# Full-array matmuls written as four tiles of 32 columns, and the last 64-row block of a down projection moved behind the scores

## The chip, the cores and the metric

The kernel runs on one core of one Trainium2 chip. The metric is the device time of one execution in microseconds (us); the kernel before takes 3293.29 us, the median of 6 runs between 3290.56 and 3295.43. The engines are named as in the profile: PE (TensorE, the matrix unit), DVE (VectorE), ACT (ScalarE), POOL (GpSimd) and SP (SyncE, which issues most DMAs). PEld is the loading of weights into PE's array, SPq is SP's queue.

## The reference

Two blocks follow each other on x of shape (8, 1024, 256), all in fp32. The first is attention with compressed keys and values. The second, which the change touches, is a two-layer transformer with attention in windows of 128 tokens:

```python
def _layer(x, wqkv, qs, ksc, wo, lg, lb, w1, b1, w2, b2):
    b, n, _ = x.shape
    h = shift_token(x)                      # second half of the features comes from the token before
    q, k, v = jnp.split(h @ wqkv, 3, axis=-1)
    q, k, v = (to_heads(q), to_heads(k), to_heads(v))   # 8 heads of 64
    q = l2norm(q) * qs
    k = l2norm(k) * ksc
    q, k = rotary_xpos(q, k)
    o = local_attention(q, k, v)            # each window sees itself and the one before
    x = x + o.transpose(0, 2, 1, 3).reshape(b, n, INNER) @ wo
    h = layernorm(shift_token(x)) * lg + lb
    a, g = jnp.split(h @ w1 + b1, 2, axis=-1)
    return x + (a * gelu(g)) @ w2 + b2      # hidden width 682 = 5 x 128 + 42
```

## The kernel before

The first phase (to about 967 us) computes the first block and leaves its result in DRAM (`x2d`). It already writes its dense products through a helper `times` (L199 to L201), which makes four matmuls of 32 output partitions each out of one product. The second phase, the function `local`, holds the two layers.

`local` makes 16 passes, one for each layer and batch row, layer 0 for all eight rows first. A pass has NT = 8 windows of 128 tokens and two chunks of CH = 512 tokens. One loop over steps (`for step in range(windows + LAG)`) advances everything by one window, and the order in which PE, DVE, ACT and POOL get their instructions is the order in which this loop emits them (`manual_schedule`). SP's order is left to a scheduler. In step `step`, in this order:

- `both` (window step - 4, L983): DVE adds the exponentials of two windows for the softmax sums.
- `qk` (window step, L886): the query and key products, 2 x 2 matmuls of 128 x 512 into one of two double banks (`pair`). ACT squares them, DVE and POOL apply the rotary tables and the norms.
- `transposes` (window step - 1, L926): DVE transposes blocks, and SP writes them to DRAM (`z`) and reads them back into the ring `qkT`.
- `v` (L913): the value product, into a bank of the pool `mm`, copied out by ACT.
- a unit of the MLP, `next(units)`
- `ahead`: on the last windows of a pass, the next pass's stream of x is loaded and, in layer 0, normalised by DVE (L788).
- `values` (window step - 4): the products with the exponentials, `o` (L999), and their sums `s` (L1007, in a bank of `mm`), both in tiles of 32 columns. DVE then takes the reciprocal of s (L1011), reduces s over its free axis for a check (L1015), scales o (L1016) and reduces the reciprocal (L1020).
- `scores` (window step - 3, L958): tiles of 64 rows and 32 columns into the two `pair` banks; ACT takes the exponentials (L964), POOL masks them.
- `output` in every second step: the output projection `psw` (L1032) into a bank of `mm`, added to x by DVE (L1036), stored by SP.
- a second unit of the MLP

The MLP of a chunk has eight units, so it takes four steps. The first five hold the up projection (`up`, L1115, tiles `ag`), with gelu on ACT and the gate on DVE (L1128, tile `hid`). The sixth makes the last 42 hidden columns: their gate and value share one product, and the result is laid in `rest_hid` as two blocks of 64 rows (L1142), one for each half of the chunk. The seventh is the down projection: `sums`, two banks of `mm`, gather 40 products over the five full blocks (L1156) and then the products with the two 64-row blocks (L1162). DVE adds both banks to x (L1168), and SP stores x, in layer 0 to `xs` (L1170). In layer 1, DVE adds the input `xt` first (L1174), and SP stores to `out`. The eighth scales the next chunk.

The pool `psum3`, tag `mm`, has three banks. A new tile gets a bank that is free in the order of the program, and its first matmul waits until the last reader of the old tile has finished. The seventh unit falls on the place between `v` and `values`, so the order in such a step is: pair, pv, psy with its rest, o, s, scores, psw.

Of the kernel before, what the change touches and what calls it, by code (L numbers as in the profile page):

```python
# [32 lines left out]
ALU = mybir.AluOpType  # L33
# [3 lines left out]
P = 128  # L37
# [20 lines left out]
DEPTH, HEADS, DH, WINDOW = 2, 8, 64, 128  # L58
INNER = HEADS * DH
# [3 lines left out]
CH = 512  # L63
# [19 lines left out]
def preln_mla_local_kernel(  # L83
# [27 lines left out]
    nc = tc.nc  # L111
# [541 lines left out]
    ST = CH // P  # L653
    NF = HID // P
# [3 lines left out]
    def local(ctx: ExitStack, verdict):  # L658
# [4 lines left out]
        p1 = ctx.enter_context(tc.tile_pool(name="l1", bufs=1))  # L663
        p2 = ctx.enter_context(tc.tile_pool(name="l2", bufs=2))

        ppair = [ctx.enter_context(tc.tile_pool(name="pair0", bufs=1, space=PSUM))]
        psum = ctx.enter_context(tc.tile_pool(name="psum3", bufs=3, space=PSUM))
        ppair.append(ctx.enter_context(tc.tile_pool(name="pair1", bufs=1, space=PSUM)))
# [7 lines left out]
        rest_hid = p1.tile([P, CH // 2], F32, name="rest_hid")  # L676
# [90 lines left out]
        def load_x2(b, n):  # L767
            xt = p1.tile([P, ST, D], F32, tag="x2", name=f"x2_{b}_{n}")
            nc.sync.dma_start(xt, x2d[b][:, ST * n : ST * n + ST])
            return xt  # L770
# [94 lines left out]
        class Pass:  # L865
# [14 lines left out]
            def qk(self, i):  # L880
                key, w = self.key(i), self.w
                A, S = w["cos"], w["sin"]
                qk = next(turns).rearrange("p (n j) (m d) -> p n (j m) d", n=2, d=DH)
                for n in range(2):
                    for c in range(2):
                        nc.tensor.matmul(  # L886
                            qk[:, n].rearrange("p h d -> p (h d)"), self.left(i)[c],
                            w["qkv"][:, c, n * INNER : (n + 1) * INNER], start=(c == 0), stop=(c == 1),
                        )
                sq = p1.tile([P, 2, HEADS, DH], F32, tag="sq", name=f"sq{key}")  # L890
                nc.scalar.activation(sq, qk, AF.Square)  # L891
                t1 = p1.tile([P, 2, HEADS, DH], F32, tag="t1", name=f"t1{key}", bufs=2)
                nc.vector.tensor_tensor(t1, qk, A[:, i].unsqueeze(2).to_broadcast([P, 2, HEADS, DH]), ALU.mult)  # L893
                t2 = p1.tile([P, 2, HEADS, DH], F32, tag="t2", name=f"t2{key}")
                for lo, hi in ((0, H), (H, 0)):
                    nc.vector.tensor_tensor(  # L896
                        t2[:, :, :, lo : lo + H], qk[:, :, :, hi : hi + H],
                        S[:, i, :, lo : lo + H].unsqueeze(2).to_broadcast([P, 2, HEADS, H]), ALU.mult,
                    )
                nc.gpsimd.tensor_tensor(t1, t1, t2, ALU.add)  # L900
                ss = small.tile([P, 2, HEADS], F32, tag="ss", name=f"ss{key}")
                nc.vector.tensor_reduce(ss, sq, AX.X, ALU.add)
                nc.vector.tensor_scalar(ss, ss, 1e-24, None, ALU.max)
                rn = small.tile([P, 2, HEADS], F32, tag="rn", name=f"rn{key}")
                rsqrt(rn.rearrange("p i h -> p (i h)"), ss.rearrange("p i h -> p (i h)"), 2 * HEADS)
                nc.gpsimd.tensor_tensor(t1, t1, rn.unsqueeze(3).to_broadcast([P, 2, HEADS, DH]), ALU.mult)  # L906
                self.rot[i] = t1

            def v(self, i):
                key = self.key(i)  # L910
                pv = psum.tile([P, INNER], F32, tag="mm", name=f"pv{key}")
                for c in range(2):
                    nc.tensor.matmul(  # L913
                        pv, self.left(i)[c], self.w["qkv"][:, c, 2 * INNER :], start=(c == 0), stop=(c == 1)
                    )
                self.vs[i] = p1.tile([P, INNER], F32, tag="v", name=f"v{key}", bufs=6)
                evac(self.vs[i], pv)

# [105 lines left out]
            def output(self, n):  # L1024

                oT = self.oTs.pop(n)
                x_, y, key = self.x_, self.y, f"{self.b}_{self.l}"
                two = slice(2 * n, 2 * n + 2)
                ps = psum.tile([P, 2, D], F32, tag="mm", name=f"psw{key}_{n}")
                for i in range(2):  # L1030
                    for c in range(4):
                        nc.tensor.matmul(  # L1032
                            ps[:, i, :], oT[:, c, i * P : (i + 1) * P], self.w["o"][:, c, :],
                            start=(c == 0), stop=(c == 3),
                        )
                nc.vector.tensor_tensor(x_[:, two], ps, x_[:, two], ALU.add)  # L1036

                rows = slice(2 * n * P, (2 * n + 2) * P)
                nc.sync.dma_start(y[rows, :P].rearrange("(t p) d -> p t d", p=P), x_[:, two, :P])
                rows = slice(2 * n * P + 1, (2 * n + 2) * P + 1)  # L1040
                nc.sync.dma_start(y[rows, P:].rearrange("(t p) d -> p t d", p=P), x_[:, two, P:])
                m, o = divmod(2 * n + 2, ST)
                if o == 0:
                    self.hs[m - 1] = p2.tile([P, ST, D], F32, tag="h", name=f"h{key}_{m - 1}")
                    rows = slice((m - 1) * CH, m * CH)
                    nc.sync.dma_start(self.hs[m - 1], y[rows].rearrange("(t p) d -> p t d", p=P))
# [2 lines left out]
        made = {}  # L1049
        chunks = [(n, m) for n in range(len(passes)) for m in range(NCH)]  # L1050
        ds, found = {}, {}

        def look_at_chunk(k):
            if k < len(chunks):
# [41 lines left out]
        def mlp():  # L1096


            w = load_mlp(0)
# [7 lines left out]
            for k, (q, n) in enumerate(chunks):  # L1107
# [4 lines left out]
                def up(i):  # L1112
                    ps = psum.tile([P, CH], F32, tag="mm", name=f"ag{key}_{i}")
                    for c in range(2):
                        nc.tensor.matmul(  # L1115
                            ps.rearrange("p (s a t) -> p s a t", a=4, t=32), w["1"][:, c, i, :],
                            d[:, c],
                            start=(c == 0), stop=(c == 1),
                        )
                    return ps  # L1120

# [24 lines left out]
                norm_chunk(k + 1)  # L1146
                turn_chunk(k + 1)
                yield
                if l + 1 == DEPTH:
                    xt = load_x2(b, n)  # L1150
                sums = [psum.tile([P, 2, D], F32, tag="mm", name=f"psy{key}_{g}") for g in range(2)]
                for g, ps in enumerate(sums):
                    for t in range(2):
                        cols = slice((2 * g + t) * P, (2 * g + t + 1) * P)
                        for i in range(NF):
                            nc.tensor.matmul(  # L1156
                                ps[:, t, :], hid[:, i, cols], w["2"][:, i, :], start=(t == i == 0), stop=False
                            )
                for t in range(2):
                    for g, ps in enumerate(sums):  # L1160
                        rows = slice(64 * g, 64 * g + 64)
                        nc.tensor.matmul(  # L1162
                            ps[:, t, :], rest_hid[rows, t * P : (t + 1) * P], w["2"][rows, NF, :], start=False,
                            stop=(t == 1),
                        )
                for g, ps in enumerate(sums):
                    part = slice(ST * n + 2 * g, ST * n + 2 * g + 2)
                    nc.vector.tensor_tensor(x_[:, part], ps, x_[:, part], ALU.add)  # L1168
                    if l + 1 < DEPTH:
                        nc.sync.dma_start(xs[b][:, part], x_[:, part])  # L1170
                    else:
                        rows = slice(n * CH + 2 * g * P, n * CH + (2 * g + 2) * P)
                        both = xt[:, 2 * g : 2 * g + 2]
                        nc.vector.tensor_tensor(both, x_[:, part], both, ALU.add)  # L1174
                        nc.sync.dma_start(out[b, rows].rearrange("(t p) d -> p t d", p=P), both)
                yield
                if k + 1 < len(chunks) and made[chunks[k + 1][0]].l > l:
                    w = load_mlp(l + 1)
# [26 lines left out]
        def each(step, name, back):  # L1205
            j = step - back
            if 0 <= j < windows:
                n, i = divmod(j, NT)
                getattr(made[n], name)(i)

        E = mybir.EngineType
        with tc.manual_schedule(engines={E.PE, E.DVE, E.Activation, E.Pool}):
            for step in range(windows + LAG):
# [18 lines left out]
                    ahead(n + 1)  # L1232
                each(step, "values", 4)
                each(step, "scores", 3)
                j = step - 6
                if 0 <= j < windows and j % 2 == 0:
                    made[j // NT].output(j % NT // 2)
# [8 lines left out]
                if i >= NT - 5 and step < windows:  # L1246
                    got = ahead(n + 1)
                    if got:
                        ready[n + 1] = got
            for _ in units:  # L1250
                pass

        ok = p1.tile([P, 2, B * DEPTH * NT], F32, name="okl")
        for m, top in enumerate((HIGH, 1 / LOW)):
# [612 lines left out]
```

## Time and profile before

| | |
|---|---|
| median of 6 runs | 3293.29 us |
| the profiled execution | 3296.12 us |
| its span, first to last instruction | 3294.3 us |
| granted clock of PE, mean | 0.993 |
| PE busy | 3199.9 us (97%), 33762 matmuls |
| DVE busy | 2668.8 us (81%) |
| ACT, POOL busy | 1711.9 us (52%), 1342.8 us (41%) |

Matmuls of the second phase that the change touches (a product in fp32 is two instructions on PE, so each product counts twice):

| line | tile | form | count | mean ns of one |
|---|---|---|---|---|
| L1115 | ag | 128\*128, 512 wide | 1408 | 597 |
| L886 | pair (qk) | 128\*128, 512 wide | 1024 | 601 |
| L913 | pv | 128\*128, 512 wide | 512 | 592 |
| L1156 | psy | 128\*128, 256 wide | 1280 | 379 |
| L1032 | psw | 128\*128, 256 wide | 1024 | 390 |
| L1162 | psy, rest | 64\*128, 256 wide | 256 | 402 |

How to read it: a form such as 128\*32 is rows times columns of the array that a matmul uses. The time of one matmul holds its way through the array, and the next one starts before it ends; what counts is therefore the distance from one start to the next. In an answer in order of time a line has the start in us, the length in us, the engine, the line of code, the operation, output and inputs, and how many instructions were merged. In brackets stands the engine's idle time just before, and what ended it. An answer by stretches has, for each, its length and then busy time and number of instructions of PE, PEld, DVE, ACT and POOL, the granted clock, the share of DMA and the GB/s.

### The profile page before, as it was taken

How to read it: one execution, taken by the hardware profiler on the slowest of the kernel's cores; microseconds unless marked ns; L12 is line 12 of the kernel's file. 1: busy time of each engine (PE TensorE's matmuls, PEld its weight loads, DVE VectorE, ACT ScalarE, POOL GpSimd, SP SyncE). 2: the span in 40 equal slices, each digit the busy share in tenths (PEclk: the TensorE clock that was granted, in tenths of full speed). 3: DMA queues.
4: the chain of work that ended last, by engine and by line, in shares of the span. 5: the costliest groups of instructions: out<-in, count | busy, mean ns of one | idle time of the engine just before them, and what ended most of it. 6: DMA issues, size and time to landing. Idle time of an engine off the chain costs nothing.

```text
span 3294.3 us, 79693 instructions
## 1 busy us (share of the span) xinstructions
PE 3199.9 (97%) x33762; PEld 1765.4 (54%) x33762; DVE 2668.8 (81%) x3934; ACT 1711.9 (52%) x2055; POOL 1342.8 (41%) x1064
## 2 busy tenths in 40 slices
PE   7999999999987999999999999999999999999998
PEld 2434343443334566656666666566665656665665
DVE  4999989998987887887878877787877778787773
ACT  6888888888742344444343444443444444444441
POOL 1000000000017655555555555555555555555540
PEclk9999999999998999999999999999999999999999
DMA  4133222313333344444445445444544535454431
GB/s 127 45 93 83 59 75 75 91 47 84 107 90 110 100 126 119 134 116 120 122 117 133 115 128 144 125 125 140 146 125 122 137 114 133 132 140 124 113 102 58
DMA packets 389771, 362.10 MB, mean 110 GB/s; under 512 B 158703, under 2 KB 337310, under 8 KB 389278
## 3 DMA queue, kind: packets, MB, share of 16 engines
q1 hardware_dynamic: 387422, 354.51, 39.7%
q8 instruction: 268, 4.39, 0.6%
q10 hardware_dynamic: 1984, 2.41, 0.2%
q14 instruction: 97, 0.79, 0.1%
HBM read 165.96 MB, written 140.51 MB: 93 GB/s over the span
## 4 chain that ended last, share of the span: by engine, by line
PE 83%; DVE 7%; ACT 4%; DMA 2%; issue 2%; SPq 1%; POOL 0%; ACTq 0%; DVEq 0%
PE ag L1115 17%; PE pair L886 13%; PE psy L1156 8%; PE psw L1032 7%; PE o L999 6%; PE pv L913 6%; PE acc L488 6%; PE sc L455 4%; PE pair L958 4%; DVE pt L477 4%; PE s L1007 2%; PE psx L201 1%; PE psR L201 1%; PE psq L201 1%; ACT pt L463 1%
## 5 line engine op out<-in xcount | busy, mean ns | idle before, releaser
L477 DVE TENSOR_TENSOR pt<-pt,er 128x1024 f32<-128x1024 f32 x576 | 671.8, 1221 | 35.6 <-ACT pt L463 35.6
L1115 PE MATMUL ag<-d,l 128*128 128x512 f32 x1408 | 640.4, 597 | 1.6 <-ACT d L1090 1.1
L900 POOL TENSOR_TENSOR t<-t,t 128x1024 f32<-128x1024 f32 x128 | 302.0, 2360 | 794.4 <-DVE t L896 794.4
L463 ACT ACTIVATE pt<-sc 128x1024 f32<-128x1024 f32 x576 | 561.2, 1033 | 115.7 <-PE sc L455 106.1
L964 ACT ACT_TABLE_LOAD x120 | 154.0, 1283 | 701.5 <-PE pair L958 701.4
L886 PE MATMUL pair<-l_qkv,xT 128*128 128x512 f32 x1024 | 469.1, 601 | 5.3 <-DMA xT<-zx 2.3
L1115 PEld LDWEIGHTS ag<-d,l 128*128 128x128 f32 x1408 | 262.2, 190 | 310.5 <-issue 276.9
L126 POOL TENSOR_TENSOR rn<-ss,half 128x16 f32<-128x16 f32 x128 | 373.4, 2917 | 13.8
L488 PE MATMUL acc<-pt,v 128*32 128x512 f32 (+3 forms) x3072 | 345.7, 496 | 11.1 <-DVE pt L477 9.9
L886 PEld LDWEIGHTS pair<-l_qkv,xT 128*128 128x128 f32 x1024 | 193.8, 192 | 248.7 <-issue 207.5
L891 ACT ACTIVATE sq<-pair 128x1024 f32<-128x1024 f32 x128 | 131.0, 1023 | 332.5 <-issue 262.4
L893 DVE TENSOR_TENSOR t<-pair,l_cos 128x1024 f32<-128x1024 f32 x128 | 156.3, 1221 | 156.9 <-ACT sq L891 156.2
L1156 PE MATMUL psy<-l,hid 128*128 128x256 f32 x1280 | 281.5, 379 | 0.0
L1128 DVE SCALAR_TENSOR_TENSOR hid<-ag,l_b,ge 128x512 f32<-128x512 f32 x160 | 116.0, 725 | 197.2 <-ACT ge L1127 171.9
L1156 PEld LDWEIGHTS psy<-l,hid 128*128 128x128 f32 x1280 | 243.2, 190 | 46.7 <-issue 15.1
L964 ACT ACTIVATE pt<-pair 128x1024 f32<-128x1024 f32 (+1 forms) x256 | 235.0, 968 | 57.7 <-PE pair L958 56.3
L906 POOL TENSOR_TENSOR t<-t,rn 128x1024 f32<-128x1024 f32 x128 | 249.1, 1946 | 10.0
L455 PE MATMUL sc<-q,k 32*128 32x512 f32 (+3 forms) x3072 | 244.9, 380 | 4.5 <-ACT pt L463 3.6
L999 PEld LDWEIGHTS o<-pt,v 128*32 128x32 f32 x7680 | 201.6, 110 | 86.4 <-issue 82.7
L1032 PE MATMUL psw<-l_o,oT 128*128 128x256 f32 x1024 | 241.9, 390 | 0.0
L913 PE MATMUL pv<-l_qkv,xT 128*128 128x512 f32 x512 | 240.6, 592 | 0.0
L455 PEld LDWEIGHTS sc<-q,k 32*128 32x128 f32 x3072 | 134.0, 183 | 195.1 <-ACT pt L463 132.4
(324 smaller groups left out, 4709.5 us busy)
## 6 DMA issues: line engine op xcount, KB each, us to landing
z<-turned SPq DMA_DIRECT2D x512, 128.0 KB, 2.4
qkT<-z SPq DMA_DIRECT2D x128, 512.0 KB, 3.6
y<-xs SPq DMA_DIRECT2D x128, 128.0 KB, 2.9
h<-y SPq DMA_DIRECT2D x32, 512.0 KB, 4.3
zx<-turneds SPq DMA_DIRECT2D x120, 128.0 KB, 2.4
xT<-zx SPq DMA_DIRECT2D x240, 64.0 KB, 2.4
zh<-turnedh SPq DMA_DIRECT2D x120, 128.0 KB, 2.3
d<-zh SPq DMA_DIRECT2D x30, 512.0 KB, 3.2
```

What stands on the lines that cost most here:

```text
L126: nc.gpsimd.tensor_tensor(out_, in_, half[:, :n], ALU.pow)
L455: nc.tensor.matmul(two[n // 2][:, n % 2, lo : lo + w], k[rows], q[rows, h], start=(h == 1), stop=(h == 0),)
L463: nc.scalar.activation(pt, sc, AF.Exp, scale=SCALE)
L477: nc.vector.tensor_tensor(t, t, er.to_broadcast([P, 1024 // w, w]), ALU.mult)
L488: nc.tensor.matmul(self.acc[g][32 * n : 32 * n + 32, q0 - c * 512 :], self.v[:, kb, h * VW : h * VW + 32], pts[n // 2][:, n % 2, lo : lo + w],
L886: nc.tensor.matmul(qk[:, n].rearrange("p h d -> p (h d)"), self.left(i)[c], w["qkv"][:, c, n * INNER : (n + 1) * INNER], start=(c == 0), s ...
L913: nc.tensor.matmul(pv, self.left(i)[c], self.w["qkv"][:, c, 2 * INNER :], start=(c == 0), stop=(c == 1))
L964: nc.scalar.activation(pt[:, :, : n * P], flat[:, :, : n * P], AF.Exp, scale=-1.0)
L999: nc.tensor.matmul(o[32 * j : 32 * j + 32, g, a, :], vs[m][:, h * DH + a * 32 : h * DH + a * 32 + 32], pts[m][g][:, place(j), off : off + ...
L1032: nc.tensor.matmul(ps[:, i, :], oT[:, c, i * P : (i + 1) * P], self.w["o"][:, c, :], start=(c == 0), stop=(c == 3),)
L1115: nc.tensor.matmul(ps.rearrange("p (s a t) -> p s a t", a=4, t=32), w["1"][:, c, i, :], d[:, c], start=(c == 0), stop=(c == 1),)
L1156: nc.tensor.matmul(ps[:, t, :], hid[:, i, cols], w["2"][:, i, :], start=(t == i == 0), stop=False)
```

## The change

Every product of the second phase that used all 128 columns goes through a helper `times`, which makes four matmuls of 32 columns out of it: qk, v, the output projection, the up projection and the down projection. The products with the 64-row blocks are split in the same way and, with the adds and stores behind them, put into a function `rest`, which is not called at once but kept in the list `rests`. The loop calls it directly behind `scores` of the same step, ahead of `output`. The load of `xt` stays where it was.

```diff
+        QUARTER = [slice(32 * n, 32 * n + 32) for n in range(4)]
+
+        def times(out, w, rhs, start, stop):
+            for four in QUARTER:
+                nc.tensor.matmul(out[four], w[:, four], rhs, start=start, stop=stop)
...
                 for n in range(2):
                     for c in range(2):
-                        nc.tensor.matmul(
+                        times(
                             qk[:, n].rearrange("p h d -> p (h d)"), self.left(i)[c],
-                            w["qkv"][:, c, n * INNER : (n + 1) * INNER], start=(c == 0), stop=(c == 1),
+                            w["qkv"][:, c, n * INNER : (n + 1) * INNER], c == 0, c == 1,
                         )
...
                 for c in range(2):
-                    nc.tensor.matmul(
-                        pv, self.left(i)[c], self.w["qkv"][:, c, 2 * INNER :], start=(c == 0), stop=(c == 1)
-                    )
+                    times(pv, self.left(i)[c], self.w["qkv"][:, c, 2 * INNER :], c == 0, c == 1)
...
                     for c in range(4):
-                        nc.tensor.matmul(
-                            ps[:, i, :], oT[:, c, i * P : (i + 1) * P], self.w["o"][:, c, :],
-                            start=(c == 0), stop=(c == 3),
-                        )
+                        times(ps[:, i, :], oT[:, c, i * P : (i + 1) * P], self.w["o"][:, c, :], c == 0, c == 3)
...
                     for c in range(2):
-                        nc.tensor.matmul(
-                            ps.rearrange("p (s a t) -> p s a t", a=4, t=32), w["1"][:, c, i, :],
-                            d[:, c],
-                            start=(c == 0), stop=(c == 1),
+                        times(
+                            ps.rearrange("p (s a t) -> p s a t", a=4, t=32), w["1"][:, c, i, :], d[:, c],
+                            c == 0, c == 1,
                         )
...
                         for i in range(NF):
-                            nc.tensor.matmul(
-                                ps[:, t, :], hid[:, i, cols], w["2"][:, i, :], start=(t == i == 0), stop=False
+                            times(ps[:, t, :], hid[:, i, cols], w["2"][:, i, :], t == i == 0, False)
+                def rest(w=w, sums=sums, l=l, b=b, n=n, x_=x_, xt=xt):
+                    for t in range(2):
+                        for g, ps in enumerate(sums):
+                            rows = slice(64 * g, 64 * g + 64)
+                            times(
+                                ps[:, t, :], rest_hid[rows, t * P : (t + 1) * P], w["2"][rows, NF, :], False, t == 1
                             )
-                for t in range(2):
                     for g, ps in enumerate(sums):
-                        rows = slice(64 * g, 64 * g + 64)
-                        nc.tensor.matmul(
-                            ps[:, t, :], rest_hid[rows, t * P : (t + 1) * P], w["2"][rows, NF, :], start=False,
-                            stop=(t == 1),
-                        )
-                for g, ps in enumerate(sums):
-                    part = slice(ST * n + 2 * g, ST * n + 2 * g + 2)
-                    nc.vector.tensor_tensor(x_[:, part], ps, x_[:, part], ALU.add)
...
+                        part = slice(ST * n + 2 * g, ST * n + 2 * g + 2)
+                        nc.vector.tensor_tensor(x_[:, part], ps, x_[:, part], ALU.add)
...
+                rests.append(rest)
...
                 each(step, "values", 4)
                 each(step, "scores", 3)
+                while rests:
+                    rests.pop()()
                 j = step - 6
                 if 0 <= j < windows and j % 2 == 0:
                     made[j // NT].output(j % NT // 2)
```

In the code after the change, matmuls of all these products carry the line of `times` (L670), the scores are L962, o L1003, s L1011, and DVE's rows of a step are L1015 (reciprocal), L1019 (reduction of s), L1020, L1024, L1166 (adds of psy) and L1037 (add of psw).

More of the change, by code (lines that the diff above doesn't have):

```diff
@@ L1051, in local @@
         ds, found = {}, {}
+        rests = []
         def look_at_chunk(k):
@@ L1148, in mlp @@
                 yield
-                if l + 1 == DEPTH:
-                    xt = load_x2(b, n)
+                xt = load_x2(b, n) if l + 1 == DEPTH else None
                 sums = [psum.tile([P, 2, D], F32, tag="mm", name=f"psy{key}_{g}") for g in range(2)]
@@ L1158, in mlp @@
                             )
-                for t in range(2):
                     for g, ps in enumerate(sums):
-                        rows = slice(64 * g, 64 * g + 64)
-                        nc.tensor.matmul(
-                            ps[:, t, :], rest_hid[rows, t * P : (t + 1) * P], w["2"][rows, NF, :], start=False,
-                            stop=(t == 1),
-                        )
-                for g, ps in enumerate(sums):
-                    part = slice(ST * n + 2 * g, ST * n + 2 * g + 2)
[L1168 to L1175, printed above, removed]
+                        part = slice(ST * n + 2 * g, ST * n + 2 * g + 2)
@@ new lines, in rest @@
+                        nc.vector.tensor_tensor(x_[:, part], ps, x_[:, part], ALU.add)
+                        if l + 1 < DEPTH:
+                            nc.sync.dma_start(xs[b][:, part], x_[:, part])
+                        else:
+                            rows = slice(n * CH + 2 * g * P, n * CH + (2 * g + 2) * P)
+                            both = xt[:, 2 * g : 2 * g + 2]
+                            nc.vector.tensor_tensor(both, x_[:, part], both, ALU.add)
+                            nc.sync.dma_start(out[b, rows].rearrange("(t p) d -> p t d", p=P), both)
@@ L1249, in local @@
                         ready[n + 1] = got
+                while rests:
+                    rests.pop()()
             for _ in units:
-                pass
+                while rests:
+                    rests.pop()()
         ok = p1.tile([P, 2, B * DEPTH * NT], F32, name="okl")
```

## Prediction

> **What bounds the kernel now.** First the chain of waits, for the engine that sets the end; then the busy time by stretches, for whether that engine ever waits in the second phase.
>
> ```profile
> PE 83%; DVE 7%; ACT 4%; DMA 2%; issue 2%; SPq 1%; POOL 0%; ACTq 0%; DVEq 0%
> ...
> 1100.00:3216.00 2116.00, 2111.62 (x21896) 1296.40 (x21897) 1681.73 (x2655) 883.91 (x952) 1164.21 (x862) 1.00 0.46 125
> ```
>
> From 1100 to 3216 us the PE (first pair of numbers after the length) is busy 2111.6 of 2116.0 us, and its largest wait there is one of 1.80 us. So the second phase is a stream of matmuls. It changes only if the PE's own time changes or if the PE begins to wait. Third, the order of time, for one step with the down projection (PE alone):
>
> ```profile
> 2009.02 8.80 PE L1156 MATMUL psy<-l,hid 128*128 128x256 f32 x40
> 2017.75 1.13 PE L1162 MATMUL psy<-l,rest_hid 64*128 64x256 f32 x8
> 2018.81 1.96 PE L999 MATMUL o<-pt,v 128*32 128x128 f32 x64
> 2020.58 0.62 PE L1007 MATMUL s<-both,ones_l 128*32 128x128 f32 x16
> 2021.13 1.32 PE L958 MATMUL pair<-qkT 64*32 64x160 f32 x64
> 2022.38 3.72 PE L1032 MATMUL psw<-l_o,oT 128*128 128x256 f32 x16
> ```
>
> The array changes shape four times here: 128\*128, 64\*128, 128\*32, 64\*32, 128\*128. A step without the block L1162 has three changes.
>
> **Streaming, old form against new.** The 40 matmuls of L1156 take 8.80 us with the last one's own 0.38, so 39 starts are (8.80-0.38)/39 = 0.216 us apart. The first phase already runs products as four tiles:
>
> ```profile
> 524.40 1.04 PE L201 MATMUL psq<-xnT,wqnat 128*32 128x512 f32 x8
> 527.88 1.91 PE L201 MATMUL psx<-wout,oT 128*32 128x256 f32 x32
> ```
>
> 32 matmuls are 8 sets of four: (1.91-0.38-0.02)/7 = 0.216 us per set. The 512-wide line is two sets: 1.04-0.59-0.02 = 0.43, as L1115 (8 in 3.60 us, the last 0.59: 3.01/7 = 0.43). Four times the instructions therefore stream in the same time; I take 0 for this. The only other sign is the mean over shorter runs of the first phase, up to 3% more (0.222), but those runs hold waits of their own.
>
> **What a change of shape costs.** (a) From the last start plus its streaming to the next start. The last psy starts at 2009.02+8.80-0.38 = 2017.44 and streams until 2017.65; L1162 starts at 2017.75: 0.09. L1162 to L999: last start 2018.50, streamed until 2018.72, next 2018.81: 0.09. L1115 to L999 (523 ns between starts instead of 429): 0.09. From scores the eight tiles of a set start 47 ns apart, and from the first of them the change takes 0.14. (b) The first weights are not hidden: after a change the first 128-column set lasts 0.320 instead of 0.216 (16 psw: 3.72-0.38 = 3.34 = 0.320+14 x 0.216), 0.104 more; the first 32-column set 0.133 instead of 0.109, 0.024 more.
>
> **What the edit takes away.** (1) Up projection to values, 93 steps: no change any more, 0.094+0.024 = 0.118 each, 11.0 us. (2) Scores to what follows, about 120: the change stays, its first weights are 32 columns, 0.104-0.024 = 0.080 each, 9.6 us. No row shows 64\*32 to 128\*32, so the ends are 0 (weights as wide as now) and 0.104; the first-phase sets after another 32-row shape begin with 0.453 instead of 0.429, again 0.024, so I take 0.080. In every fourth step the pair products wait for ACT's exponentials (657 ns between starts instead of 429), which swallows the 0.080, but the pair's first set after that wait loses its 0.104 too. (3) The rest, 31 times: it enters behind scores in the same 64-row, 32-column shape, so its two changes and their weights go: 0.09+0.104+0.09+0.024 = 0.317, 9.8 us. Its four streams of 0.216 stay. Sum: 30.4 us less.
>
> **What the edit adds: a wait of psw.** The banks of the pool `mm` are three. Psy holds two of them; formerly until the two adds L1168, which ran beside the values. Now the adds come behind the scores, and s has the third bank. So psw of that step gets the bank of s, and its first weight load waits for the last reader of s, the reduction L1015, behind the reciprocal. All PE work of the next steps is queued behind it. Old DVE rows beside the excerpt above:
>
> ```profile
> 2021.27 1.76 DVE L1011 RECIPROCAL rs<-s 128x256 f32<-128x256 f32 x1 [1.07 <-PE s L1007]
> 2022.94 0.36 DVE L1015 TENSOR_REDUCE stats<-s 128x1 f32<-128x256 f32 x1
> ```
>
> I count from the last psy start (2017.44). Old: values 1.37, last s start 3.49, reduction's end 5.86, which is 2.37 behind s; psw 4.94. New: values at 0.22, last s at 2.31, so the reduction ends at 4.68 and psw may start at 4.74 (a wait of the first phase's kind ends 0.05 after its DVE row). Scores run 2.51 to 3.54, the four rest sets begin at 3.63, and psw would be ready at 3.63+4x0.216+0.14 = 4.63. Wait 0.11, in 10 chunks. In the second chunk of a pass the scores are shorter (1.11 us), psw is ready at 4.42, wait 0.33, in 15 chunks. Together 6.1 us.
>
> In six chunks of the first layer DVE is late, because the next pass is normalised there:
>
> ```profile
> 1168.94 1.29 DVE L926 STREAM_TRANSPOSE turned<-t 128x512 f32<-128x512 f32 x2
> 1170.17 1.24 DVE L1168 TENSOR_TENSOR xs<-psy,xs 128x512 f32<-128x512 f32 x2
> 1171.34 2.94 DVE L788 TENSOR_SCALAR xs<-xs,mvs,rstds 128x256 f32<-128x256 f32 x4
> 1174.21 1.74 DVE L1011 RECIPROCAL rs<-s 128x256 f32<-128x256 f32 x1
> 1175.87 0.35 DVE L1015 TENSOR_REDUCE stats<-s 128x1 f32<-128x256 f32 x1
> ```
>
> Today psw starts at 1171.09, before L1015 has run, and nobody minds. Without the adds L788 starts at 1170.17. Its four take 1.34 us at 1159.34; the 2.94 here has a fourth that lasts 2 us and ends with POOL's L906 (1172.18 to 1174.13). Now they would be through at 1171.51, ahead of L906, which hangs on earlier DVE rows. Reciprocal 1171.44, reduction's end 2.01 later, 1173.45, plus 0.05, plus 0.20 that the PE has gained since DVE last idled: psw at 7.55 after the last psy (1166.15), where 4.63 was possible. Wait 2.92 each, 17.5 us.
>
> **The clock.** After the one wait of 1.80 us the granted clock (the number before the last two) fell:
>
> ```profile
> 2047.52:2050.93 3.41, 1.60 (x73) 1.08 (x68) 0.00 (x0) 0.40 (x1) 0.00 (x0) 1.00 0.72 234
> 2050.94:2054.35 3.41, 3.41 (x8) 2.75 (x9) 1.96 (x4) 2.82 (x3) 1.43 (x3) 0.50 0.14 24
> ```
>
> That took 1.7 us (psw 5.41 instead of 3.72). A stretch with 1.62 us of idle PE (1064.49 to 1067.90, 1.79 busy) kept the full clock. I take 1.7 us of idle in one stretch of 3.41 as the point from which the clock falls. A wait of 2.9 us misses it only where a stretch's border cuts it between 1.2 and 1.7 us from its start, 0.5 of 3.41, 15% of positions. The loss is half of the next stretch, less half of what the wait still fills of it, 1.6 us on average: 0.85x1.6 = 1.35 each, 8.1 us. The ends are 0 and 6x1.7 = 10.2.
>
> The Trainium skill ("TensorE: Matmul & The Clock Gate", HAM oscillation) asks for gaps over about 3.4 us before the clock is throttled; by it these 2.9 us would cost nothing and the sum would be 8 us lower. The 1.80 us wait above contradicts it, and the trace decides.
>
> Other moved work: DVE's adds, and in layer 1 the two adds of `xt`, run up to 4 us later, before psw's own add at about 8.5; the stores from SP are held, and the next qkT load (issued 5.8 after psy) stands behind one of them by 0.5 us. Its scores come two steps later, some 35 us. All free; uncovered, 0.5 us a chunk, 16 us. Every other wait of PE in the steady stretch has at least 1.79 us to spare (ag L1115 on DVE L1128 is the nearest), apart from the pair products on the exponentials, which part (2) holds.
>
> **Sum.** -30.4+6.1+17.5+8.1 = +1.3 us. The profiled execution took 3296.12 (span 3294.3), 2.8 above the median of 3293.29, to which I add: 3294.6.
>
> **Rivals.** *The clock stays full (faster):* the six waits come but no stretch is idle enough, or the waits are shorter: 3286.5 without the clock term, 3280 with two thirds of the waits. For it: 1.07 us at 3221 passed unpunished. Against: 2.92 is far over 1.80. 3276 to 3287.
> *DVE and POOL collide again (slower):* if the fourth L788 starts after L906, as today, the reciprocal stays at 1174.2 and psw starts at 10.3: 2.75 us more in six places, and the clock falls nearly always (+2): 3313. It decides at a margin of 0.67 us (1171.51 against 1172.18).
> *Tiles in series:* if hi and lo passes of a tile ran before the next tile, each product would take up to four times as long. The products stream for (1408+1024+512)x0.429+(1280+1024)x0.216 = 1760 us now, so this would be milliseconds. The L201 rows exclude it.
>
> **Numbers.** A measurement here tells about 0.2% (6.6 us) from no change. Forecast 41% (3287 to 3300), clock stays 28%, collision or another longer wait 30%, the last rival 1%. So faster 0.28, same 0.41, slower 0.31. The forecast's own range is 3287 to 3300; with both signs 3277 to 3313.
>
> **What would show it.** Right: psy followed by o without a gap; sets 0.216 and 0.43; psw waiting for DVE L1019 0.1 to 0.3 us in most chunks and about 2.9 us in six, with the clock at half behind most of these. Wrong: sets of four slower than 0.22, no wait before psw, a fourth normalise of 2 us again, or PE waiting for qkT.

## The result and the profile after

| | before | changed |
|---|---|---|
| median | 3293.21 us (40 runs, 3290.33 to 3298.99) | 3299.73 us (20 runs, 3292.56 to 3306.49) |
| ratio, 95% interval | | 1.0018 (1.0012 to 1.0024) |
| the profiled execution, its span | 3296.12, 3294.3 us | 3303.34, 3301.6 us |
| PE busy | 3199.9 us | 3179.6 us |
| instructions on PE | 33762 | 50274 |

The ratio is within 0.2%, which counts as no difference here, but its interval leaves out 1: the change costs some 6 us. PE has 20 us less to do, and gets none of it, since it now waits. The stretch from 1100 to 3216 us, by engine (PE, PEld, DVE, ACT, POOL busy, then granted clock, DMA share, GB/s):

```profile
1100.00:3216.00 2116.00, 2084.09 (x36989) 1036.57 (x36984) 1656.76 (x2640) 884.65 (x952) 1166.05 (x862) 0.99 0.46 126
```

Before, PE was busy for 2111.62 of these 2116 us. Of the 32 us that are idle now, the waits of PE in the same stretch name the larger part (total, times, longest):

```profile
PE psw L670 <- DVE stats L1019: 22.1, 18, 3.0
PE s L1011 <- DVE both L987: 2.6, 1, 2.6
PE pair L962 <- DMA qkT<-z: 0.8, 1, 0.8
PE psy L670 <- issue: 0.6, 1, 0.6
```

("issue" stands for a pause for which the profile names no cause. Pauses of under 0.15 us, such as the one of psw in the next rows, are too short for this list.)

One step in order of time shows what the tiles do (PE alone; 160 matmuls of psy where there were 40):

```profile
2025.18 8.82 PE L670 MATMUL psy<-l,hid 128*32 128x256 f32 x160
2033.82 1.93 PE L1003 MATMUL o<-pt,v 128*32 128x128 f32 x64
2035.56 0.62 PE L1011 MATMUL s<-both,ones_l 128*32 128x128 f32 x16
2036.11 1.32 PE L962 MATMUL pair<-qkT 64*32 64x160 f32 x64
2037.22 1.07 PE L670 MATMUL psy<-l,rest_hid 64*32 64x256 f32 x32
2038.43 1.93 PE L670 MATMUL psw<-l_o,oT 128*32 128x256 f32 x32
```

Psy takes as long as before (8.80), o follows one set (0.216) behind its last start, and the rest enters the stream 0.09 behind the last score. Then psw should start some 0.3 behind the last set of the rest. It starts at 2038.43, which is 4.81 behind the last psy start (2033.62). The end of DVE's reduction of s says why: in 26 of the 30 chunks that have a psw behind their rest, psw starts 0.145 to 0.147 behind it (in three later, in one 0.100).

The same step in one of the six chunks where the next pass is normalised (PE, then DVE):

```profile
1163.22 1.93 PE L1003 MATMUL o<-pt,v 128*32 128x128 f32 x64
1164.96 0.62 PE L1011 MATMUL s<-both,ones_l 128*32 128x128 f32 x16
1165.51 1.32 PE L962 MATMUL pair<-qkT 64*32 64x160 f32 x64
1166.62 1.07 PE L670 MATMUL psy<-l,rest_hid 64*32 64x256 f32 x32
1170.73 2.79 PE L670 MATMUL psw<-l_o,oT 128*32 128x256 f32 x24 [3.03 <-DVE stats L1019]
```

```profile
1166.08 1.29 DVE L930 STREAM_TRANSPOSE turned<-t 128x512 f32<-128x512 f32 x2
1167.30 1.33 DVE L794 TENSOR_SCALAR xs<-xs,mvs,rstds 128x256 f32<-128x256 f32 x4
1168.56 1.74 DVE L1015 RECIPROCAL rs<-s 128x256 f32<-128x256 f32 x1
1170.22 0.35 DVE L1019 TENSOR_REDUCE stats<-s 128x1 f32<-128x256 f32 x1
```

The sums s are ready at 1165.6; their reciprocal starts at 1168.56, because DVE works without a pause through the rows before it. The fourth normalise no longer collides with POOL (1.33 for the four, not 2.94). And the clock (stretches around this wait; the number before the last two is the granted clock):

```profile
1166.37:1169.78 3.41, 1.32 (x64) 0.74 (x47) 3.41 (x7) 3.30 (x4) 3.33 (x2) 1.00 0.44 100
1169.78:1173.20 3.42, 2.47 (x24) 1.36 (x28) 2.91 (x6) 1.44 (x2) 3.42 (x6) 0.50 0.27 84
1173.20:1176.61 3.41, 3.41 (x36) 1.81 (x32) 0.00 (x0) 0.00 (x0) 0.33 (x1) 0.50 0.87 271
```

The measure that I use below is the distance from one chunk's first psy to the next one's. A pass has two chunks, so the distances come in pairs:

| | layer 1 (steady) | first chunk of a pass, layer 0 | across the change of layer |
|---|---|---|---|
| before | 71.48 + 70.40 | 71.48 | 75.22 |
| changed | 70.70 + 69.83 | 76.47, 75.02, 75.28, 75.01, 75.28, 73.60 | 76.31 |
| tiles only | 70.79 + 69.71 | 70.86 to 70.88 | 75.91 |
| changed, s ahead of o | 70.49 + 69.46 | 73.59 to 75.28 | 75.47 |
| the best version | 70.49 + 69.46 | 70.86 to 70.89 | 74.48 |

### The profile page after: what moved, and what is told of

Its sections match the earlier page's. It is cut to its first block, busy times and chain, and to the rows that moved or that the text cites. A ratio compares the mean times of both kernels' runs of the same rounds, so it can differ in the third digit from the quotient of the medians.

```text
span 3301.6 us, 112747 instructions
## 1 busy us (share of the span) xinstructions
PE 3179.6 (96%) x50274; PEld 1490.6 (45%) x50274; DVE 2652.0 (80%) x3934; ACT 1712.8 (52%) x2055; POOL 1346.9 (41%) x1064
## 4 chain that ended last, share of the span: by engine, by line
PE 53%; DVE 5%; issue 1%; ACT 1%; DMA 0%; SPq 0%; DVEq 0%; ACTq 0%
PE ag L670 15%; PE pair L670 11%; PE psy L670 7%; PE psw L670 6%; PE pv L670 5%; PE o L1003 5%; PE pair L962 3%; PE s L1011 1%; DVE rs L1015 1%; ACT pt L968 1%; DVE turned L930 0%; DVE xs L794 0%; ACT L968 0%; DVE bnsts L783 0%; SPq L850 0%
## 5 line engine op out<-in xcount | busy, mean ns | idle before, releaser
L670 PE MATMUL ag<-d,l 128*32 128x512 f32 x5632 | 640.4, 593 | 0.6 <-ACT d L1086 0.4
L670 PE MATMUL pair<-l_qkv,xT 128*32 128x512 f32 x4096 | 466.4, 594 | 6.8 <-DMA xT<-zx 1.8
L670 PEld LDWEIGHTS ag<-d,l 128*32 128x32 f32 x5632 | 184.9, 110 | 377.8 <-issue 353.6
L670 PE MATMUL psy<-l,hid 128*32 128x256 f32 x5120 | 282.2, 379 | 0.0
L670 PEld LDWEIGHTS pair<-l_qkv,xT 128*32 128x32 f32 x4096 | 136.6, 110 | 301.7 <-issue 247.6
L670 PE MATMUL psw<-l_o,oT 128*32 128x256 f32 x4096 | 249.4, 397 | 23.8 <-DVE stats L1019 22.4
L1015 DVE RECIPROCAL rs<-s 128x256 f32<-128x256 f32 x128 | 223.1, 1743 | 47.4 <-PE s L1011 47.4
L1003 PEld LDWEIGHTS o<-pt,v 128*32 128x32 f32 x7680 | 216.9, 110 | 64.4 <-issue 55.0
L670 PE MATMUL pv<-l_qkv,xT 128*32 128x512 f32 x2048 | 244.3, 592 | 0.0
L1003 PE MATMUL o<-pt,v 128*32 128x128 f32 x7680 | 235.2, 273 | 1.7 <-POOL pt L970 1.6
```

The costliest lines, as they stand in the source:

```text
L670: nc.tensor.matmul(out[four], w[:, four], rhs, start=start, stop=stop)
L1003: nc.tensor.matmul(o[32 * j : 32 * j + 32, g, a, :], vs[m][:, h * DH + a * 32 : h * DH + a * 32 + 32], pts[m][g][:, place(j), off : off + ...
L1015: nc.vector.reciprocal(rs, s)
```

## The experiments

Nine kernels were run, 5 to 11 times each. The kernel before ran beside them and had medians of 3295.39 us (first four), 3293.82 (next three) and 3292.60 (last two); ratios are to these.

| | median, us | ratio to before, 95% interval |
|---|---|---|
| tiles only, rest in its old place | 3279.48 | 0.9952 (0.9938 to 0.9965) |
| move only, full-array products | 3316.86 | 1.0068 (1.0055 to 1.0082) |
| changed, normalising behind the rest | 3289.76 | 0.9984 (0.9975 to 0.9993) |
| changed, s ahead of o | 3293.65 | 0.9997 (0.9988 to 1.0006) |
| changed, normalising half a step earlier | 3296.35 | 1.0005 (0.9996 to 1.0014) |
| the same, s ahead of o | 3287.46 | 0.9981 (0.9972 to 0.9990) |
| tiles only, 64 columns wide | 3291.16 | 0.9990 (0.9981 to 0.9999) |
| s ahead of o, rest moved only where DVE is free | 3270.01 | 0.9935 (0.9922 to 0.9949) |
| changed, half of the normalising left out | 3274.97 | 0.9943 (0.9929 to 0.9957) |

**The two halves of the change, each alone.** Tiles only:

```diff
-                rests.append(rest)
+                rest()
```

> All full products as four tiles, the rest block back in its old place between the down projection and the values. Theory (tiles save changes of shape, and the move loses by psw's wait for the bank of s, at 31 places): no psw wait of more than 0.1 us is left, no clock drop between 1100 and 2020 us, and the savings stand alone: 93 x 0.118 + 120 x 0.080 = 20.6 us, and of the 31 x 0.317 of the rest block only the first weights, some 31 x 0.1 = 3 us: 3293.2 - 23.7 = 3269.5, taken as 3268 to 3274, with the runs as close together as those of the kernel before (8 us). Rival (the tiles themselves cost time: four times the instructions, their supply or their streaming): over 3280, with the scatter of 14 us kept.

Move only:

```diff
         def times(out, w, rhs, start, stop):
-            for four in QUARTER:
-                nc.tensor.matmul(out[four], w[:, four], rhs, start=start, stop=stop)
+            nc.tensor.matmul(out, w, rhs, start=start, stop=stop)
```

> The rest block behind the scores, all products as one full array again. Theory (the bank wait is the price of the move): short waits of 0.1 to 0.27 in 25 chunks (about 5 us), six of about 2.9 (17.7), the clock at half behind most of them (8), and the layer change 1.7 worse: 3293.2 + 32 = 3326, range 3318 to 3330. Rival (the tiles eat their own gain, the move costs little): 3293 to 3303.

Measured: the tiles take 15.9 us off, the move puts 21.5 on. The sum, 5.6, is what the whole change does (ratio 1.0018, 5.9 us). So the tiles are a gain and the move a loss, and neither rival holds; but both sizes were overrated, and both times lie outside the ranges expected. The step of "tiles only":

```profile
2296.76 1.09 PE L670 MATMUL psy<-l,rest_hid 64*32 64x256 f32 x32
2297.79 1.95 PE L1003 MATMUL o<-pt,v 128*32 128x128 f32 x64
2299.56 0.62 PE L1011 MATMUL s<-both,ones_l 128*32 128x128 f32 x16
2300.11 1.32 PE L962 MATMUL pair<-qkT 64*32 64x160 f32 x64
2301.35 3.66 PE L670 MATMUL psw<-l_o,oT 128*32 128x256 f32 x64
```

There is no wait ahead of psw, and the rest to o takes 1.03 (before: 2017.75 to 2018.81, 1.06). But the changes of shape have not become cheaper. Psy to rest is 0.329 from start to start and rest to o 0.326, where the 128-column forms took 0.309 and 0.306: taking off a set each, the two changes cost 0.22. Of the 0.1 that I gave the rest for narrower first weights (31 x 0.1 = 3 us) little is left: its first set does last 0.240 instead of 0.320, but the two changes take most of this back, and from the last psy to o it is 1.353 instead of 1.373. A pair in layer 1 takes 140.50 against 141.88, so 15.5 pairs give 21 us. Some of it is then lost: 1.3 us at the change of layer (75.91 is 5.05 over 70.86; before, 3.74), and in pauses for which no cause is named, on which more at the end.

The waits of "move only":

```profile
PE psw L669 <- DVE stats L1018: 14.6, 6, 2.4
PE pair L961 <- DMA qkT<-z: 1.8, 1, 1.8
```

The six long waits are there and the clock fell behind four of them (2.49, 4.17, 4.16, 4.18, 2.48 and 4.16 us over 71.48, together 21.6, nearly the whole loss). The short waits of the expectation are only partly there. In every chunk but one psw starts 0.146 to 0.148 behind the reduction, as in the changed kernel. In a second chunk of a pass this is 0.21 later than the products would allow, too short a pause for the list, and the chunk lasts 70.59 instead of 70.40. In a first chunk of layer 1 it is 0.01: there psw comes just when the bank is free.

**Whether the six long waits are DVE's backlog.** First the normalising goes behind the rest in the order of instructions:

```diff
-                if NT - 2 <= i and step < windows:
-                    ahead(n + 1)
                 each(step, "values", 4)
                 each(step, "scores", 3)
                 while rests:
                     rests.pop()()
+                if NT - 2 <= i and step < windows:
+                    ahead(n + 1)
```

> The changed kernel with the next pass's normalising emitted behind values, scores and rest instead of ahead of them; nothing else. Theory: the reciprocal of s is no longer late in six chunks, so the six waits of 3.0 us become 0.2 like the others, and the clock drops behind them go: 3299.7 - 6 x 2.9 - 5 x 1.5 = 3275, range 3270 to 3280. Rival (what is late is the adds and stores of the rest, or DVE as a whole, so that pushing the normalising back only moves the wait): 3290 or more, with waits of over 1 us elsewhere in the same six steps.

Between the two: some 11 us better than the changed kernel by the ratios, not 25. The waits of this kernel:

```profile
PE psw L670 <- DVE stats L1019: 13.2, 16, 1.8
```

Six are still long, five of 1.73 to 1.76 us and one of 1.48. The reciprocal now comes straight behind the transposition, 4.27 behind the last psy, where 2.63 is on time: DVE was behind already when the step began, by the first normalising, the statistics and the rest of its queue. I had counted only the last of these blocks. No clock drop followed any of the six.

Then all three blocks half a step earlier, and the same with s ahead of o:

```diff
-                if NT - 2 <= i and step < windows:
+                if i in (NT - 3, NT - 1) and step < windows:
                     ahead(n + 1)
```

> The changed kernel with the next pass's first normalising, second statistics and second normalising half a step earlier each, so that the step of the rest block begins with less of them left for DVE. Theory (the six long waits are DVE's backlog of normalising AND statistics in front of the reciprocal of s): reciprocal 2.6 us behind the last psy in all chunks, the six waits 0.2 like the others, no clock drop behind them: against the changed kernel 6 x 2.85 + 5 x 1.5 = 24.6 us less, 3293 + 6.4 - 24.6 = 3275, range 3271 to 3280. Rival (DVE has no room: the backlog only moves, since the second normalising now waits for GpSimd's square root right behind the statistics): waits of over 1 us remain or come up at other lines, 3285 or more.

> The same, and the matmuls of s ahead of those of o. Theory: no wait of psw is left at all, so that the tiles and the move keep what they save: 7.7 us less than the kernel with earlier normalising alone, 3267, range 3264 to 3273, below the version with tiles only (3277.5 by the same reference) by the two changes of shape of the rest, 31 x 0.22 = 7 us, and up to 3 more. Rival (the PE, earlier now, waits for DMAs instead, as it does at the change of layer): 3273 to 3280, with waits on qkT, d or the products' inputs.

The rival of the first, that DVE has no room, holds in both. The backlog moved and made a second wait: psy, which opens the step, now waits for the bank of the s of the step before. From the first of the two:

```profile
PE psw L670 <- DVE stats L1019: 14.1, 17, 2.0
PE psy L670 <- DVE stats L1019: 5.3, 6, 0.9
```

The rival of the second, new waits for DMAs, does not: its list of waits names none. S ahead of o is worth 7.9 us between the two (0.9981 against 1.0005).

So the amount of DVE's work was tried, not its place. Half of the normalising, that of the second half of a pass's rows, is left out in layer 0 from the second batch row on, so that this kernel computes something else:

```diff
                 normalise(xs_[:, parts[0]], found[0])
-                found.append(statistics(xs_[:, parts[1]], f"s{b}_1"))
+                if b == 0:
+                    found.append(statistics(xs_[:, parts[1]], f"s{b}_1"))
...
-                if l == 0 and n == ((l, b) == (0, 0)):
+                if (l, b) == (0, 0) and n == 1:
                     normalise(xs_[:, parts[1]], found[1])
```

> The changed kernel, with the statistics and the normalising of the second half of a pass's rows left out in the first layer from the second batch on, so that DVE has some 3.7 us less to do ahead of the six late reciprocals; nothing else. Theory (the long waits of psw are this backlog and nothing else): the six waits shrink from 3.0 to 0.2 us and no clock drop follows; against the changed kernel 6 x 2.8 + 5 x 1.5 = 24 us less: 3299.7 - 24 = 3275 where the kernel before takes 3293.2, range 3271 to 3279. Rival (the backlog is only a part; the later adds and stores of the rest cost in these steps too): waits of over 0.5 us remain in the six steps, 3283 or more.

3274.97 us, as expected. Its waits on the reduction:

```profile
PE psw L670 <- DVE stats L1020: 3.6, 12, 0.3
```

The first chunks of a pass take 70.70 to 70.75 in layer 0 too. The six waits with the clock drops behind them cost 5.9 + (3292.60 - 3274.97) = 23.5 us, and they are DVE's backlog; nothing of the adds and stores that moved with the rest shows in these steps.

**Whether psw waits for s.** The matmuls of s go ahead of those of o, in the changed kernel:

```diff
+                for g in range(2):
+                    for j in range(4):
+                        nc.tensor.matmul(
+                            s[32 * j : 32 * j + 32, g, :], ones, self.sums[g][:, place(j), :], start=True, stop=True
+                        )
                 for g in range(2):
                     for a in range(2):
                         for m, off in blocks:
...
```

> The changed kernel with the matmuls of s issued ahead of those of o inside the values; nothing else. Theory (psw waits for the last reader of the bank of s): the reciprocal starts 1.75 us earlier, the short waits of 25 chunks (0.20 in 10, 0.37 in 15: 7.6 us) vanish, the six long ones stay at 3.0, because there DVE is busy with the normalising until 5.5 us after the last psy: 3299.7 - 7.6 = 3292, range 3288 to 3296. Rival (psw waits for something else, or the waits are a pipeline cost of the change of shape): 3298 to 3301, with psw still 0.5 us or more behind the last rest matmul in every chunk.

0.9997 against the changed kernel's 1.0018 is 6.9 us, and 7.6 was expected. In all 24 other chunks psw now starts 0.30 to 0.31 behind the last start of the rest, where the changed kernel mostly has 0.52 or 0.68. DVE in a steady chunk, whose last psy starts at 2312.8:

```profile
2313.83 1.71 DVE L1015 RECIPROCAL rs<-s 128x256 f32<-128x256 f32 x1
2315.47 0.35 DVE L1019 TENSOR_REDUCE stats<-s 128x1 f32<-128x256 f32 x1
```

The reduction ends at 2315.82 and psw starts at 2317.71, when the stream of PE reaches it. The six long waits stayed at 3.0. That the bank of s is what psw waits for is shown by this: nothing but the time of s was changed, and psw followed.

**Whether it is the shape, or the cutting, that saves.** Tiles only, with two tiles of 64 columns:

```diff
-        QUARTER = [slice(32 * n, 32 * n + 32) for n in range(4)]
+        QUARTER = [slice(64 * n, 64 * n + 64) for n in range(2)]
```

> As the version with tiles only, but two tiles of 64 columns in place of four of 32. Theory (what is saved is the change of shape between neighbours in the stream, and the first weights behind one): the up projection to values goes back to 0.52 between starts, the first set behind scores lasts longer than 0.24 again, so at most the shorter first weights (about 0.05 each, 120 x 0.05 = 6 us) are kept: 3287 to 3296 where the kernel before takes 3293. Rival (cutting a product into tiles saves time by itself, whatever their width): 3276 to 3281, as with 32.

Of the 15.9 us some 3 are left (0.3 to 6.3 by the interval). The up projection to values is back at 0.522 from start to start (0.523 with full arrays, 0.429 with 32 columns), so the tiles save by having their neighbours' shape.

**A version that keeps both gains.** S goes ahead of o as above, and the rest moves only where DVE is not normalising:

```diff
-                rests.append(rest)
+                if l or n:
+                    rests.append(rest)
+                else:
+                    rest()
```

> The matmuls of s ahead of those of o, and the rest block behind the scores only where DVE is not busy with the next pass: in the second layer and in the second chunk of a pass; in the first chunks of the first layer it stays in its old place. Theory (the move is worth its two changes of shape, 0.11 each, wherever psw finds a free bank): no psw wait on DVE; two chunks together take 70.49 + 69.46 us in the second layer (tiles only: 70.79 + 69.71) and 70.9 + 69.46 in the first; against tiles only 15 x 0.27 + 8 x 0.25 = 6 us less, 3277.4 - 6 = 3271 where the kernel before takes 3293.2, range 3268 to 3275. Rival (the stream is bound elsewhere by now, at the change of layer and by the supply of instructions, as the misses of 'tiles only' against its forecast suggest): no gain over tiles only, 3276 to 3281.

3270.01 us, 0.9935 of the kernel before (0.9922 to 0.9949) and 0.9917 of the changed one by the two ratios; 3268 to 3275 was expected. Against the tiles alone (0.9952) the two intervals overlap; that it is the better one is read from the distances, 139.95 a pair in layer 1 instead of 140.50. The waits of PE from 1100 to 3216 us:

```profile
PE s L1000 <- DVE both L987: 2.3, 1, 2.3
PE psy L670 <- issue: 0.9, 2, 0.6
PE ag L670 <- ACT d L1086: 0.4, 1, 0.4
PE pair L670 <- ACT pt L968: 0.4, 1, 0.4
PE pair L962 <- DMA qkT<-z: 0.4, 1, 0.4
```

## Why the prediction was right, and where it was not

The forecast was +1.3 us and the change measures +5.9: right in mechanism, some 5 us short. Its range was 3287 to 3300 and the median is 3299.73, so the upper end was just enough. Single executions of the changed kernel spread over 14 us.

- **Streaming.** Held: 0.216 and 0.429 between sets, psy 8.82 against 8.80. But "I take 0 for this" left something out: pauses of PE without a named cause (below).
- **Changes of shape, (1) and (2).** Held. Up projection to o is 0.429 instead of 0.523, and the sets behind scores lose most of their longer start. (The 47 ns of the prediction lie between the first and the last of a set's eight tiles.) "Tiles only" and the 64-column kernel show that this is the change of shape.
- **The rest, (3).** Held for the move, as its two changes of shape are gone. (Its four terms, as printed, add up to 0.308 and not 0.317; that is 0.3 us in all.) What the move is worth shows only where psw does not wait: s ahead of o and the moved rest together take 0.55 off a pair (139.95 against 140.50), and no run has the move without a wait and with o first.
- **Short waits of psw.** The mechanism held; each was about 0.1 longer. I let psw start 0.05 behind DVE's row, from a wait of the first phase; it starts 0.146 behind it: the first weight load 0.115, the matmul another 0.03. That is 3 us over 30 chunks. In the steady pairs the sum was near all the same: 1.52 less was predicted, 1.35 came (140.53 against 141.88).
- **Six long waits.** 3.01 to 3.04 for 2.92, at the six chunks named; the extra is the same 0.1. The fourth normalise ran ahead of POOL's row, so the slower rival did not come.
- **The clock.** It fell behind five of the six, for 85% predicted. The first chunks of the passes lie 26.5 us over six times 70.70; 17.4 is waits over the short ones, and 9.1 is left for the clock (8.1 predicted, one fall lasted two stretches). How near this came is partly luck: with s ahead of o, waits of the same length made it fall behind three of the six.
- **What failed.** "All free", of the moved adds and stores and of PE's other waits, and "every other wait has at least 1.79 us to spare": at the change of layer PE waits 2.60 for DVE's `both` and 0.81 for qkT, where it waited 1.80, and this chunk lies 5.61 over its like instead of 3.74. That is 1.9 us. Part of it is there with the tiles alone (5.05): PE comes earlier to a transfer that does not. How much the held stores add is open, as no run moved them by themselves. Whether the clock falls there differs, too: it did in nine of the eleven profiles.
- **What was not in the sum.** Other chunks of the changed kernel hold together 2.3 us that their like do not, of which 0.8 shows as idle put down to "issue" (0.6 and 0.2).

With 0.9 for long waits and clock, 1.9 and 2.3, these terms come to 5.1, as much as lies between the forecast and the two profiles' +6.3 (at the start of the last down projection). That this fits so well is in part chance. The 0.17 that each steady pair falls short, some 2.5 us in all, has to be added. Against it stands the stretch from the end of the first phase to the first psy, which took 188.2 us in the changed profile and 191.2 in the one before; in the eleven profiles it ranges from 186.7 to 194.0, whichever the kernel. So the account is closed to some 3 us, not better.

## What to carry to other kernels

A product cut into tiles of its neighbour's shape streams as fast as a whole one and saves the change of shape, 0.12 us a time here; two tiles of 64 columns, which do not meet the neighbour's shape, save little. Moving work on the bounding engine is a question of banks: ask which buffer the next instruction will get, and who reads that buffer last, for an engine at 80% with a burst in its queue is late just there. Where such a wait is short and comes from the reader's position, moving the reader's input earlier removes it (s ahead of o: all the short waits, none of the long ones). Shifting the other engine's queue made the long waits here shorter, 3.0 to 1.7 or 2.0, but carried part of the backlog to another place; not moving the rest where DVE is busy avoided them.

## What the runs showed that was not expected

**PE pauses in the middle of a product, perhaps for want of instructions.** From the profile, the queue that brings instructions; before and then changed:

```profile
q8 instruction: 268, 4.39, 0.6%
```

```profile
q8 instruction: 397, 6.50, 0.8%
```

In one chunk of the changed kernel:

```profile
1677.86 0.65 PE L670 MATMUL psy<-l,rest_hid 64*32 64x256 f32 x9
1679.07 1.06 PE L670 MATMUL psy<-l,rest_hid 64*32 64x256 f32 x23 [0.56 <-issue]
```

Such gaps in the middle of a product, for which no semaphore is named, make up 0.6 to 2.1 us in seven of the eight kernels with 32-column tiles. The eighth, with half of the normalising left out, the full-array kernels (two) and the 64-column one show none of over 0.15 us. They return at nearly the same places of PE's program whatever the order around them: near matmul 21983 in four of the kernels, near 29495 in five, at 40696 in two. They lie in or behind the scores and the rest, where starts are closest (64 score tiles start within 1.1 us, 160 of psy in 8.4). That the supply of instructions is the cause fits this, but was not tried by itself, and the eighth kernel takes the same 397 packets without such a gap.

**The clock falls for idle time well under its stretch of 3.41 us.** Behind waits of about 3.0 us it fell in 5 of 6 cases and, with s ahead of o, 3 of 6; behind 2.4 us in 4 of 6; behind 1.95 to 1.98 in 2 of 10 (both kernels with earlier normalising, which have two more of 1.02); behind 1.48 to 1.76 in none of 6. It matters how the wait lies in the stretches. In the changed kernel the wait of 3.0 us that ends at 1897.9 lies across a border of two stretches, 1.96 before it and 1.08 behind, and costs nothing more. (Counted from the falls of the clock, which all lie on a grid of 3.41 us, the border is at 1896.82; the rows below begin 0.11 earlier.)

```profile
1893.30:1896.71 3.41, 1.56 (x76) 0.98 (x61) 3.41 (x8) 3.09 (x3) 3.22 (x3) 1.00 0.34 72
1896.71:1900.12 3.41, 2.22 (x44) 1.66 (x48) 3.16 (x6) 1.65 (x3) 3.41 (x6) 1.00 0.35 89
1900.12:1903.54 3.42, 3.42 (x51) 1.71 (x47) 1.92 (x5) 0.00 (x0) 0.58 (x1) 1.00 0.99 272
```

In "move only" a stretch with 2.04 us of idle time was followed by half the clock, one with 1.91 was not, while the 1.7 that I took as the border came from one fall in the kernel before. The border lies near 2 us of idle time in one stretch and is not sharp: 1.80 was followed by half the clock in the kernel before, 1.98 was not with s ahead of o.
